# First mixture of a one-core transformer block: row scatters two to a step over eight steps, one more step ahead of the routing product, head attention in smaller parts

## The chip, the core and the metric

The kernel runs on one core of one Trainium2 chip, in fp32. The metric is device time in microseconds for one execution. Within the core the work is spread over five engines: TensorE (PE, with its weight load shown as PEld), VectorE (DVE), ScalarE (ACT), GpSimd (POOL) and SyncE (SP, which here only issues transfers). Each engine runs its own list of instructions in the order in which the program put them; engines wait for one another through semaphores.

## The reference

Input `x` has 8 batches of 512 tokens with 256 features.

```python
x = x + attn_ref(cond_ref(x, bias, mask, ...))      # 1, 2
x = x + ffn_ref(cond2_ref(x, cond, ...))            # 3, 4

# 1 cond_ref: attention with 16 heads of 64 and one key/value head, a bias, a null key
#   and a mask (a query sees only padded keys behind it), then a layer norm
# 2 attn_ref: attention over the 16 heads of each single token
att = softmax(einsum('bthd,btgd->bthg', q, k) / 4)
out = einsum('bthg,btgd->bthd', att, v) @ Wout + bout
# 3 cond2_ref: mixture of 8 experts, the two best for each token
scores = softmax((x @ wt.T + g @ wg.T) / 2)
topk_w, topk_idx = top_k(scores, 2)                 # weights made to sum to 1
y_all = einsum('etm,emh->eth', leaky(x @ w_gate) * (x @ w_up), w_down)   # m = 128
y = sum of topk_w * y_all over the two + leaky(x @ sw_gate) * (x @ sw_up) @ sw_down
# 4 ffn_ref: attention with 16 heads of 16 over all 512 tokens, layer norm,
#   8 experts of 512, one per token, layer norm
```

## The kernel before

**Stages.** Up to some 345 us the kernel does attention 1, in which only the last 128 tokens of each batch have keys (`late_keys`); beside it, in steps, run the routing and the mixture of the first group of batches. From 389 to about 1590 us runs the main loop: attention 4 for all eight batches, with the routing, mixture and head attention of what is still missing threaded in between. From 1590 us on runs the last mixture of experts.

**The main loop.** It has 256 passes called halves, 32 to a batch. A batch has four sets of four heads, a set takes eight halves, and a half does a row tile of 128 tokens for two heads. In each half TensorE makes the score rows for two heads of the set ahead (`pss`, line 1613), whose greatest value VectorE takes (`nmz`, line 1615), and the transposed scores of the current set (`pst`, line 1637), whose exponential ScalarE takes (`pT_s`, line 1638). These tiles share four PSUM banks. `augment` (line 1628) turns the greatest values and subtracts them, once per set; `project` makes queries and keys of a later set; `gather` (`po_s`, line 1660) multiplies weights and values. `divide` takes the sums of a set to SBUF by a small transfer (`sums`, on ACT's queue), takes their reciprocal (line 1684), sends it back by another small transfer (`rr`, line 1685, on SP's queue), and two steps later spreads it with a product on TensorE (`prs`, line 1689). `end` closes a batch: projection (`px_s`), residual, and a layer norm whose power is a POOL instruction (`e_rs`, line 1712).

**Steps at the side.** Routing, mixture and the begin of the next batch are Python generators; each `yield` ends a step. A plan lists them with their number of steps and, for each batch's begin, the half by which it must be done. In every half as many steps are taken as the nearest goal asks for: 73 steps up to half 48 in the kernel before, about 1.5 a half, and 1.14 a half later.

Batches go in four groups of two (q = 0 to 3). `route(b)` works in five steps: load and turn the rows, logits (`pl_r`), softmax, the two best (`oc`, `r_o`), then a product that counts for each token how many tokens before it chose the same expert (`pr`, line 1353). `mixture(q)` makes from the counts a slot for each of the 2 × 1024 choices (line 1379), writes each token's row to its two slots with indirect transfers issued by POOL (`xs`, line 1387: 16 of them a group, each 128 rows), and fetches the weights of the first pairs of tiles (`fetch`, SP). Some steps later `rows(0)` and `rows(1)` load the sorted rows (`xg`, line 1415, on SP's queue; such a load must wait for the last scatter), and `turn`, `widen` and `narrow` run twelve pairs of tiles.

**Heads.** `late_heads` does attention 2 for the last row tile of each batch, 29 steps a batch: `products` multiplies eight blocks of two heads on POOL (line 321, four buffers), and VectorE sums each block three steps later (line 324); this is done twice, for scores and for values. The sums are pinned: VectorE runs them in program order. In the main loop four such steps are taken per half until they run out. The heads of the first batches are done beside `late_keys`.

**The order on an engine.** Instructions that are not pinned may be placed by a scheduler at compile time; on the chip the order is fixed, and an instruction that waits holds all behind it on its engine. This holds for the issue of transfers on SP's queue too.

Of the kernel before, what the change touches and what calls it, by code (L numbers as in the profile page):

```python
# [19 lines left out]
NT = S // P  # L20
# [12 lines left out]
GB = 2  # L33
TILE1_BITS = 7
TILE1 = 1 << TILE1_BITS
TILES1 = ((2 * GB * S - E) // TILE1 + E + 1) // 2 * 2
# [4 lines left out]
def tile_adaln_attn_ffn(ctx: ExitStack, tc: tile.TileContext, a: dict, out: bass.AP):  # L41

    nc = tc.nc
# [64 lines left out]
    xs_d = dram.tile([TILES1 * TILE1, D], F32, name="xs", tag="xs")  # L108
# [5 lines left out]
    with nc.allow_non_contiguous_dma(reason="narrow rows"):  # L114
# [8 lines left out]
        out=before, in_=before, pattern=[[1, P]], compare_op=ALU.is_gt, fill=0.0, base=0, channel_multiplier=-1  # L123
# [127 lines left out]
    oh_done = [0] * B  # L251
# [930 lines left out]
    def alone(dma, key, why):  # L1182

        tc.declare_no_dep(dma.ins, group=key, reason=why)
        tc.add_to_no_dep_group(key, dma.ins)
# [36 lines left out]
    with ExitStack() as ph:  # L1222
# [77 lines left out]
        def route(b):  # L1300


            q, bl = divmod(b, GB)
            if b not in x1:
                load_x1(b)
            yield
            xT = x1Ts[b] = transposed(mk, ps_m, x1[b], "x1T", bufs=2, ps_tag="m")

            nc.sync.dma_start(rows_d[b * S : (b + 1) * S, 0:D].rearrange("(t p) c -> p t c", p=P), x1[b])
            yield  # L1310
            if (b + 1) % GB:
                load_x1(b + 1)
            gb = mk.tile([64, P], F32, name="gb", tag="gb", bufs=1)
            nc.vector.tensor_copy(gb, gT[:, b : b + 1].to_broadcast([64, P]))
            pl = ps_m.tile([P, NT, E], F32, name="pl_r", tag="m")
            for t in range(NT):
                for k in range(KD):
                    nc.tensor.matmul(
                        pl[:, t, :], xT[:, k, t * P : (t + 1) * P], wtT[:, k, :], start=(k == 0), stop=False
                    )  # L1320
                nc.tensor.matmul(pl[:, t, :], gb, wgT, start=False, stop=True)
            m = mk.tile([P, NT], F32, name="r_m", tag="r_m")
            nc.vector.tensor_reduce(m, pl, AX.X, ALU.max)
            sc = mk.tile([P, NT, E], F32, name="r_sc", tag="r_sc")
            nc.vector.tensor_tensor(sc, pl, bc(m, 2, E), ALU.subtract)
            nc.scalar.activation(sc, sc, AF.Exp, scale=0.5)
            nc.vector.tensor_reduce(m, sc, AX.X, ALU.add)
            nc.vector.reciprocal(m, m)
            nc.vector.tensor_tensor(sc, sc, bc(m, 2, E), ALU.mult)
            yield  # L1330
            if bl == 0:
                chosen[q] = mp.tile([P, GB, 2, NT, E], F32, name="oc", tag="oc", bufs=2)
                ranks[q] = mp.tile([P, GB, NT, E], F32, name="rk", tag="rk", bufs=2)
            oc = chosen[q][:, bl]
            mw = sel[b] = mp.tile([P, 2, NT], F32, name=f"mw{b}", tag=f"mw{b}")
            m1 = first_max(mk, sc, rank8, "1", oc[:, 0])
            s2 = mk.tile([P, NT, E], F32, name="r_s2", tag="r_s2")
            nc.vector.scalar_tensor_tensor(s2, oc[:, 0], -2.0, sc, ALU.mult, ALU.add)
            m2 = first_max(mk, s2, rank8, "2", oc[:, 1])
            den = mk.tile([P, NT], F32, name="r_den", tag="r_den")  # L1340
            nc.vector.tensor_tensor(den, m1, m2, ALU.add)
            nc.vector.tensor_scalar(den, den, 1e-20, None, ALU.add)
            nc.vector.reciprocal(den, den)
            nc.vector.tensor_tensor(mw[:, 0], m1, den, ALU.mult)
            nc.vector.tensor_tensor(mw[:, 1], m2, den, ALU.mult)
            both_e = mk.tile([P, NT, E], F32, name="r_o", tag="r_o")
            nc.vector.tensor_tensor(both_e, oc[:, 0], oc[:, 1], ALU.add)
            yield
            sf = sofar1[:, q]
            for t in range(NT):  # L1350
                nc.vector.tensor_tensor(sf[:, t + 1, :], sf[:, t, :], both_e[:, t, :], ALU.add)
            pr = ps_m.tile([P, NT, E], F32, name="pr_1", tag="m")
            nc.tensor.matmul(pr, before, both_e, start=True, stop=False)
            nc.tensor.matmul(pr, every, sf[:, 0:NT, :], start=False, stop=True)
            nc.vector.tensor_copy(ranks[q][:, bl], pr)
            nc.vector.tensor_copy(sf[:, 0, :], sf[:, NT, :])
            yield

        PAIRS = TILES1 // 2
        WAIT = 5  # L1360

        def mixture(q):

            bank = ps_m.tile([P, E], F32, name="pn1", tag="m")
            steer, _, lead = table(mp, bank, sofar1[:, q, 0, :], TILES1, TILE1_BITS, "m_")
            rk, oc = ranks.pop(q), chosen.pop(q)
# [12 lines left out]
            nc.vector.tensor_copy(slot.rearrange("p b c t -> p (b c t)"), sf_)  # L1379
            got, xTs, hs = {}, {}, {}  # L1380

            def scatter(bl):

                xb = x1.pop(GB * q + bl)
                for c in range(2):
                    for t in range(NT):
                        sc_ = nc.gpsimd.indirect_dma_start(  # L1387
                            out=xs_d,
                            out_offset=bass.IndirectOffsetOnAxis(ap=slot[:, bl, c, t : t + 1], axis=0),
                            in_=xb[:, t, :],  # L1390
                            in_offset=None,
                            bounds_check=TILES1 * TILE1 - 1,
                            oob_is_err=False,
                        )
                        alone(sc_, f"xs{q}", "no two tokens have one place")

            def fetch(j):
                w = mk.tile([P, 2, 2, KD, P], F32, name="w_gu", tag="w_gu")
                wd = mk.tile([P, 2, D], F32, name="w_dn", tag="w_dn", bufs=3)
                for u in range(2):  # L1400
                    i = 2 * j + u
                    e = nc.sync.value_load(steer[0:1, 0, i : i + 1], min_val=0, max_val=E - 1)
                    for c, src in enumerate(("w_gate", "w_up")):
                        nc.sync.dma_start(
                            w[:, u, c], a[src][bass.ds(e, 1)].rearrange("e (k p) m -> p (e k) m", p=P)
                        )
                    nc.sync.dma_start(wd[:, u], a["w_down"][bass.ds(e, 1)].rearrange("e m d -> (e m) d"))
                got[j] = w, wd
# [40 lines left out]
                r = 2 * j * TILE1  # L1449
                nc.scalar.dma_start(y1_d[q][r : r + 2 * TILE1, :].rearrange("(u p) c -> p u c", p=P), y1)  # L1450

            scatter(0)
            fetch(0)
            yield
            scatter(1)
            fetch(1)
            for _ in range(WAIT - 1):
                yield
            rows(0)
            rows(1)  # L1460
# [192 lines left out]
        def gather(n, c):  # L1653

            b, g = divmod(n, 4)
            if c == 0:
                pos[n] = ps_o.tile([P, S], F32, name="po_s", tag="o")
            ws = [weights.pop((n, c, pr)) for pr in range(2)]
            for hd in range(4):
                nc.tensor.matmul(  # L1660
                    pos[n][hd * 32 : hd * 32 + 32, :],
                    v_sets[b % 3][:, c, (4 * g + hd) * VW : (4 * g + hd) * VW + 32],
                    ws[hd // 2][:, hd % 2, :],
                    start=(c == 0),
                    stop=(c == NT - 1),
                )
# [77 lines left out]
            if j == 7:  # L1744
                augment(0)

        ROUTE, MIX, BEGIN = 5, WAIT + 2 * PAIRS + 4, 15
        plan = []
        for q in range(B // GB):
            plan.append((64 * q + 16, begin(2 * q + 1), BEGIN))  # L1750
# [13 lines left out]
        for j in range(halves):  # L1764
            n, i, pr = half(j)
            b, g = divmod(n, 4)
            if j % 32 == 0 and b:
                last = end(b - 1)
            m, t, pm = half(j + 8 + LEAD)
            assert pm == pr  # L1770
            both(m, t, n, i, pr)
            for _ in range(4):
                next(late_heads)
            if j % 8 == 8 - LEAD and n + 1 < 4 * B:
                augment(n + 1)
            if j % 8 in (1, 2):
                if j % 8 == 1:
                    after = project(n + 2) if n + 2 < 4 * B else iter(())
                next(after, None)
            if j % 8 in (2, 3, 4, 5):  # L1780
                next(over, None)
            if j % 32 >= 6:
                next(last, None)

            due += max([(c - due) / (by - j) for by, c in goals if by > j and c > due], default=0.0)
            while done < due - 1e-6:
                assert next(side, "end") != "end"
                done += 1
            if pr == 0 and i:
                gather(n, i - 1)  # L1790
            if j % 8 == 7:
                gather(n, NT - 1)
                over = divide(n)
                next(over)
# [273 lines left out]
```

## Time and profile before

| | us |
|---|---|
| median of three runs | 1856.75 (1849.16 to 1860.49) |
| profiled execution | 1837.18 |
| its span | 1835.1 |

| engine | busy us | share of the span |
|---|---|---|
| TensorE | 1568.9 | 85% |
| VectorE | 1031.2 | 56% |
| ScalarE | 583.9 | 32% |
| POOL | 561.3 | 31% |

The mean granted TensorE clock is 0.899. The scatters of the four groups start at 256.8, 542.6, 839.3 and 1132.3 us. The first turn of rows of the mixture (`pt`, line 1423) comes at 283.3 us. The augments, one for each eight halves, come at 401.3, 455.3, 515.6, 589.1, 635.2 and 684.6 us, then 40 us apart and less. The granted clock in windows of 10 us is 0.78, 0.67, 0.50, 0.52 and 1.00 from 540 to 590 us.

How to read the lines further down: a timeline line has start and duration in us, engine, line, operation, output and inputs, shape, the number of instructions taken together, and in brackets the idle time of the engine before it and what ended it. A line of the waits has engine and line that waited, the releaser, and then total us, times, and the longest.

### The profile page before, as it was taken

Reading aid. Unit: us, or ns where it says so; the run is one execution under the profiler, and the core shown is the slowest. Engines: PE = TensorE matmul, PEld = TensorE weight load, DVE = VectorE, ACT = ScalarE, POOL = GpSimd, SP = SyncE. Lnnn points to the kernel's source line nnn. Section 1 sums busy time; section 2 is a strip of 40 time slices with the busy share of each in tenths; the row PEclk is TensorE's granted clock in tenths of the full one; section 3 lists DMA queues with packets and bytes.
Section 4 is the critical chain, followed back from the end, with each engine's and each line's share of the span. In section 5 each row is a group of like instructions: output and inputs, shape, how many; then the busy total and the mean of one; then the engine's idle time right before and its main releaser. Section 6 shows DMA issues by size and latency. Waiting matters only on the chain.

```text
span 1835.1 us, 23467 instructions
## 1 busy us (share of the span) xinstructions
PE 1568.9 (85%) x7720; PEld 880.9 (48%) x7720; DVE 1031.2 (56%) x2709; ACT 583.9 (32%) x1281; POOL 561.3 (31%) x534
## 2 busy tenths in 40 slices
PE   2897888789897999998999899899899899639995
PEld 1664656543433554443554344454433333228884
DVE  3877554356673655555545656545756656225566
ACT  0433323202222332332353332344343343203331
POOL 2444351425445433103001302201201001147775
PEclk9897788867777989998999998999999999959998
DMA  5121236701114531002850102462100000046872
GB/s 167 39 83 35 83 110 201 199 26 38 32 54 144 165 98 38 19 1 92 190 157 30 36 7 66 109 182 67 37 1 7 13 1 14 4 154 212 238 222 66
DMA packets 189460, 157.77 MB, mean 86 GB/s; under 512 B 43214, under 2 KB 173774, under 8 KB 189329
## 3 DMA queue, kind: packets, MB, share of 16 engines
q1 hardware_dynamic: 147520, 109.10, 20.7%
q0 software_dynamic: 13056, 29.67, 5.1%
q10 hardware_dynamic: 28752, 17.41, 3.2%
q8 instruction: 63, 1.03, 0.3%
q14 instruction: 69, 0.56, 0.1%
HBM read 117.00 MB, written 44.21 MB: 88 GB/s over the span
## 4 chain that ended last, share of the span: by engine, by line
PE 54%; DVE 16%; issue 14%; POOL 8%; DMA 4%; ACT 1%; SPq 0%; POOLq 0%; ACTq 0%; DVEq 0%
PE pss L1613 12%; PE po_s L1660 6%; PE pg L1433 5%; PE pq_s L1565 3%; DVE nmz L1615 3%; PE pk_s L1571 3%; POOL pr L321 3%; POOL xs L1387 3%; PE px_s L1700 2%; PE py L1446 2%; PE pst L1637 2%; PE prs L1689 1%; PE pg L1483 1%; PE pv_s L1592 1%; DMA w_gu<-in_w_up_dram 1%
## 5 line engine op out<-in xcount | busy, mean ns | idle before, releaser
L1615 DVE TENSOR_REDUCE nmz<-pss 128x1 f32<-128x512 f32 x512 | 334.3, 685 | 224.2 <-PE pst L1637 188.7
L1638 ACT ACTIVATE pT_s<-pst 128x512 f32<-128x512 f32 x512 | 282.1, 595 | 448.7 <-PE pst L1637 443.3
L1613 PE MATMUL pss<-k_s,q_s 32*128 32x512 f32 x1024 | 360.7, 682 | 42.9 <-DVE nmz L1615 42.9
L1637 PE MATMUL pst<-q_s,k_s 32*128 32x512 f32 x1024 | 339.6, 670 | 4.5 <-DVE nmz L1615 3.6
L1613 PEld LDWEIGHTS pss<-k_s,q_s 32*128 32x128 f32 x1024 | 103.9, 192 | 229.0 <-DVE nmz L1615 104.9
L1660 PE MATMUL po_s<-pT_s,v 128*32 128x512 f32 x1024 | 165.6, 633 | 8.0 <-ACT pT_s L1638 8.0
L1278 POOL DMA_INDIRECT yg<-y,slot x64 | 66.4, 1038 | 301.7 <-DMA y<-y 170.7
L321 POOL TENSOR_TENSOR pr<-qk 128x512 f32<-128x512 f32 x72 | 89.8, 1282 | 103.5 <-DVE qk L299 67.2
L1433 PEld LDWEIGHTS pg<-xT,w_gu 128*128 128x128 f32 x768 | 95.6, 201 | 40.4 <-ACT xT L1424 17.1
L1433 PE MATMUL pg<-xT,w_gu 128*128 128x128 f32 x768 | 102.7, 289 | 13.3 <-ACT xT L1424 6.9
L321 POOL TENSOR_TENSOR pr<-at,v_h 128x512 f32<-128x512 f32 x72 | 90.5, 1288 | 67.1 <-DVE at L336 38.9
L1637 PEld LDWEIGHTS pst<-q_s,k_s 32*128 32x128 f32 x1024 | 96.8, 190 | 19.6 <-DVE nmz L1615 9.5
L1387 POOL DMA_INDIRECT xs<-x,slot x64 | 63.4, 991 | 126.1 <-DVE slot L1379 108.0
L1888 PE MATMUL ph<-xTj,w 128*128 128x256 f32 x368 | 85.7, 387 | 0.0
L1211 POOL DMA_INDIRECT ids<-token_id,pi x32 | 31.7, 992 | 174.0 <-DVE pi L1208 157.8
L1902 PE MATMUL py<-w,h_e 128*128 128x256 f32 x368 | 83.5, 380 | 1.4 <-issue 1.4
L1891 ACT ACTIVATE h_e<-ph,b 128x256 f32<-128x256 f32 x92 | 43.5, 473 | 108.8 <-PE ph L1888 105.1
L1888 PEld LDWEIGHTS ph<-xTj,w 128*128 128x128 f32 x368 | 71.5, 195 | 10.3 <-ACT xTj L1876 0.2
L1438 DVE TENSOR_TENSOR hh<-hh,pg 128x256 f32<-128x256 f32 x48 | 20.2, 420 | 97.0 <-ACT hh L1437 97.0
L1902 PEld LDWEIGHTS py<-w,h_e 128*128 128x128 f32 x368 | 68.2, 190 | 10.1 <-issue 1.8
L1565 PE MATMUL pq_s<-yT,wqp 128*128 128x512 f32 x128 | 68.7, 663 | 0.9 <-DVE hh L1439 0.7
L1712 POOL TENSOR_TENSOR e_rs<-e_ve,mhalf 128x4 f32<-128x4 f32 x8 | 8.9, 1108 | 192.9 <-DVE e_ve L1710 192.7
(298 smaller groups left out, 2604.2 us busy)
## 6 DMA issues: line engine op xcount, KB each, us to landing
w<-in_w_dram SPq DMA_DIRECT2D x46, 512.0 KB
w_gu<-in_w_gate_dram SPq DMA_DIRECT2D x96, 128.0 KB
w_gu<-in_w_up_dram SPq DMA_DIRECT2D x96, 128.0 KB
w_dn<-in_w_down_dram SPq DMA_DIRECT2D x96, 128.0 KB
xg<-xs SPq DMA_DIRECT2D x48, 256.0 KB
y<-y ACTq DMA_DIRECT2D x48, 256.0 KB
rows<-xr SPq DMA_DIRECT2D x8, 544.0 KB
x<-x SPq DMA_DIRECT2D x8, 512.0 KB
```

The lines of the kernel that those rows point to most:

```text
L321: nc.gpsimd.tensor_tensor(pr, x, y, ALU.mult)
L1278: nc.gpsimd.indirect_dma_start(out=yg[t][:, c, :], out_offset=None, in_=y1_d[grp], in_offset=bass.IndirectOffsetOnAxis(ap=yi[:, c, t : t + ...
L1387: sc_ = nc.gpsimd.indirect_dma_start(out=xs_d, out_offset=bass.IndirectOffsetOnAxis(ap=slot[:, bl, c, t : t + 1], axis=0), in_=xb[:, t, :] ...
L1433: nc.tensor.matmul(pg[:, c, u, :], w[:, u, c, k, :], xT[:, k, u, :], start=(k == 0), stop=(k == KD - 1))
L1565: nc.tensor.matmul(pq, wqp[:, k, gs], yT[:, k, :], start=(k == 0), stop=(k == KD - 1))
L1613: nc.tensor.matmul(pss, qs[n][r, t * P : (t + 1) * P], ks[n][r, :], start=True, stop=True)
L1615: yield lambda: nc.vector.tensor_reduce(nmz[n % 2].rearrange("p t (h r) -> p t h r", h=4)[:, t, h, HD : HD + 1], pss, AX.X, ALU.max, negat ...
L1637: nc.tensor.matmul(pst, ks[n][r, c * P : (c + 1) * P], qs[n][r, :], start=True, stop=True)
L1638: yield lambda: nc.scalar.activation(pT[:, u, :], pst, AF.Exp)
L1660: nc.tensor.matmul(pos[n][hd * 32 : hd * 32 + 32, :], v_sets[b % 3][:, c, (4 * g + hd) * VW : (4 * g + hd) * VW + 32], ws[hd // 2][:, hd % ...
L1888: nc.tensor.matmul(ph_, w1[:, k, c * P : (c + 1) * P], xT[:, k, :], start=(k == 0), stop=(k == KD - 1))
L1902: nc.tensor.matmul(py[:, u, :], h[:, c, u * P : (u + 1) * P], w2[:, c, :], start=(c == 0), stop=(c == 3))
```

## The change

`route` gets one more `yield`, between the running sums and the counting product. `mixture` begins with a `yield` of its own. Its scatters are no longer issued in two blocks of eight (a batch each) but two to a step over eight steps (a row tile of 128 tokens with its two choices), with the weight fetches at the first and the fifth; two steps after the last scatter step, where there were four after the second block, the rows are asked for. The constants that tell the plan the number of steps follow (ROUTE 5 to 6, MIX 33 to 38). In the main loop the head steps are no longer taken four at a time ahead of the side steps: two come ahead, and behind the side steps and `gather` two more, or one more once the head of the fourth batch is done.

```diff
@@ route
                 nc.vector.tensor_tensor(sf[:, t + 1, :], sf[:, t, :], both_e[:, t, :], ALU.add)
+            yield
             pr = ps_m.tile([P, NT, E], F32, name="pr_1", tag="m")
@@
-        WAIT = 5
+        WAIT = 12
 
         def mixture(q):
 
+            yield
             bank = ps_m.tile([P, E], F32, name="pn1", tag="m")
...
-            def scatter(bl):
-
-                xb = x1.pop(GB * q + bl)
+            xb = [x1.pop(GB * q + bl) for bl in range(GB)]
+
+            def scatter(k):
+
+                bl, t = divmod(k, NT)
                 for c in range(2):
-                    for t in range(NT):
-                        sc_ = nc.gpsimd.indirect_dma_start(
...
+                    sc_ = nc.gpsimd.indirect_dma_start(
...
@@
-            scatter(0)
-            fetch(0)
-            yield
-            scatter(1)
-            fetch(1)
-            for _ in range(WAIT - 1):
+            for k in range(GB * NT):
+                scatter(k)
+                if k % 4 == 0:
+                    fetch(k // 4)
+                yield
+            for _ in range(WAIT - GB * NT - 3):
                 yield
             rows(0)
             rows(1)
@@
-        ROUTE, MIX, BEGIN = 5, WAIT + 2 * PAIRS + 4, 15
+        ROUTE, MIX, BEGIN = 6, WAIT + 2 * PAIRS + 2, 15
@@ main loop
             both(m, t, n, i, pr)
-            for _ in range(4):
+            for _ in range(2):
                 next(late_heads)
...
             if pr == 0 and i:
                 gather(n, i - 1)
+            for _ in range(1 if oh_done[2 * GB - 1] == NT else 2):
+                next(late_heads)
             if j % 8 == 7:
```

## The prediction

> **What bounds the kernel now.** I read the busy times first, then the shares of the chain that ended last, then the waits of TensorE, and last the timeline around each wait that this change touches.
>
> ```profile
> PE 1568.9 (85%) x7720; PEld 880.9 (48%) x7720; DVE 1031.2 (56%) x2709; ACT 583.9 (32%) x1281; POOL 561.3 (31%) x534
> PE 54%; DVE 16%; issue 14%; POOL 8%; DMA 4%; ACT 1%; SPq 0%; POOLq 0%; ACTq 0%; DVEq 0%
> PE pss L1613 <- DVE nmz L1615: 42.9, 43, 10.0
> PE prs L1689: 15.3, 3
> ```
>
> The last two are from the waits (us in total, times, longest) and from who waited for the DMA of line 1685. TensorE is the bound: busy 85% of 1835.1 us. A change to scatters and steps saves time only where TensorE stands still, or runs at a lower granted clock because it stood still. Its idle time in the stretch with head attention (388 to 700 us) is about 32 us. So three places matter: the scatters of group 1 (543 to 563 us), the ends of the scatters of groups 2 and 3 (860 and 1153 us), and the routing products near 500 us.
>
> Group 1, timeline of POOL, VectorE and TensorE:
>
> ```profile
> 542.59 1.05 POOL L1387 DMA_INDIRECT xs<-x,slot  x1 [0.32 <-DVE slot L1379]
> ...
> 562.15 0.98 POOL L1387 DMA_INDIRECT xs<-x,slot  x1 [0.30 <-issue]
> 563.14 6.11 POOL L321 TENSOR_TENSOR pr<-at,v_h 128x512 f32<-128x512 f32 x5
> 564.45 0.69 DVE L324 TENSOR_REDUCE oh<-pr 128x32 f32<-128x512 f32 x1 [14.70 <-POOL pr L321]
> 549.21 1.22 PE L1613 MATMUL pss<-k_s,q_s 32*128 32x512 f32 x1 [3.03 <-DVE nmz L1615]
> 565.79 1.22 PE L1613 MATMUL pss<-k_s,q_s 32*128 32x512 f32 x1 [10.04 <-DVE nmz L1615]
> ```
>
> Sixteen scatters hold POOL for 20.6 us (1.29 us from one to the next). The head's product stands behind them, the reduce of that product blocks VectorE for 14.7 us, the row maxima behind it come late, and TensorE stops for 3.0 and 10.0 us.
>
> Group 2, the chain of waits:
>
> ```profile
> 858.51 2.42 DMA xs<-x,slot
> 860.94 0.38 SPq L1415
> 861.36 0.47 SPq L1415
> 861.95 2.69 DMA rr<-sums
> 864.68 2.07 PE prs L1689 x2
> ```
>
> No heads are left here, so POOL's block itself costs nothing. But the two loads of scattered rows (L1415) wait in SP's queue for the last scatter to land, and behind them in that queue stands the small transfer of the softmax reciprocals (L1685). Those were computed at 848.6; their transfer goes out at 861.95. TensorE stands idle 4.68 us before L1689, and as long at group 3:
>
> ```profile
> 864.68 2.07 PE L1689 MATMUL prs<-rr,cst 128*128 128x512 f32 x2 [4.68 <-DMA rr<-sums]
> ```
>
> **The change, part by part.** Nothing is removed: the same 64 scatters, transfers and products are issued. What changes is their place. I read it from the order in which the changed kernel's instructions stand on each engine.
>
> *Groups 2 and 3.* POOL still gets 16 scatters in a row, since no other POOL work lies between; they start when the slots are ready and take 20.6 + 2.4 us to land. Rows(0) now comes nine side steps after the first scatter, before five: at some 1.25 steps a half (1.14 before) and 5 us a half that is 36 us instead of 22, so the loads find their rows written; and in SP's order the transfer of reciprocals now stands ahead of both. So the idle times go: 4.68 + 4.58 us. The granted clock after them was 0.75, 0.50, 0.50 and 0.55 in the four 2-us windows from 862 to 870 and 1.00 after 870: about 5.2 us of work at half clock, so 2.6 to 2.8 us lost each time. Together 7.3 + 7.4 = 14.7 us. Against it: the power of the layer norm (L1712, POOL) stood right behind the scatters at 859.5 and 1152.5 and can be the next late thing (0 to 3 us in all), and the pair weights are fetched with a slightly shorter lead. I take −12.5 (ends −14.7 and −1.5, the latter if the next wait takes nearly all of it).
>
> The Trainium skill, "TensorE: Matmul & The Clock Gate", section "The HAM clock gate", says that after an idle window of about 3.4 us the clock is halved and comes back after about 3.4 us of sustained work. By that page each of these stalls would be worth an estimated 4.6 + 1.7 = 6.3 us, and the sum below would be −12 and not −14; the trace disagrees, with 5 us at half clock here and 12 us at 0.50 to 0.52 after the 10-us stop at 566.
>
> *Group 1.* POOL's order is now 4 scatters, 3 products, 4 scatters, 2 products, 8 scatters, then products: smaller blocks, but the last is still 8 × 1.29 = 10.3 us, and on VectorE the reduce that needs the first product behind it stands directly behind the earlier reduces. POOL has 20.6 + 5 × 1.28 = 27 us of work there, in halves that took 31 us before. Going through the order by hand, VectorE waits about 5, 4 and 10 us in place of 14.7, and TensorE, which has up to four score banks of slack, about 0, 3 and 11 in place of 3 + 10 + 2. I take 0; the ends are −15 − 6 = −21 (blocks wholly covered, and some 12 us at half clock no longer lost) and +6 (a stall per block).
>
> *Group 0* runs beside late-key attention (before 388 us). The layer norm power (L89), for which VectorE waited 9.1 and 7.0 us there, no longer stands behind eight scatters at once, but the first turned rows come later: rows(0) comes six to eight side steps later, at ten steps a unit 0.6 to 0.8 unit, and the mixture starts about one group of instructions later. TensorE's turn of the rows waited 7.5 us for them before. The 12 pairs behind it take 5.1 us each, the transfer engines 82 to 99% busy. I take +3; the ends are −4 and +20 (the whole delay of the rows shows at the end of the stage).
>
> *Routing.* The product of line 1353 stood idle 6.48 us for the chosen experts, with some 2.6 us of half clock behind it:
>
> ```profile
> 502.63 0.61 PE L1353 MATMUL pr<-r_o,before 128*128 128x32 f32 x2 [6.48 <-DVE r_o L1347]
> ```
>
> It gets one more step of distance, but in TensorE's order it still stands two halves behind the logits, with fewer reduces ahead of it on VectorE. I take −4 (ends −9 and 0).
>
> *Heads.* Steps per half fall from 4 to 3 once the fourth batch's head is done (about half 7). Five heads of 29 steps end at half 36 now; (145 − 28)/3 = 39 more halves makes it 46. The work is the same: 16 × 1.28 = 20.5 us of POOL, about 14.5 us of VectorE and 4.9 us of TensorE a head. Eight halves with heads took 54.0, 60.3, 73.5, 46.0 and 49.5 us; the same stage without them took 40.1, 40.0, 43.7, 33.5 and 32.3. So heads cost 93.7 us in about 39 halves, 2.4 us a half (3.7 at worst, 29.8/8). If the cost goes with the work it is 0; I take 0 (the ends are in the rivals).
>
> Sum: −12.5 + 0 + 3 − 4 + 0 = −13.5, say −14 us on the profiled execution's 1837.2 us, −0.76%. That execution is 1.05% under the median of the runs shown, so the forecast on the median is 1856.75 × (1 − 0.0076) = 1842.6. Its own range, from the smaller ends above, is 1833 to 1853.
>
> **Rivals.**
>
> *The smaller parts really hide the scatters.* Head steps now come in two lots a half, one of them behind the side steps, so the products find POOL between the scatters. For: the 14.7-us wait of VectorE has no other cause. Against: eight scatters in a row remain in POOL's order. It would save the 21 us of group 1 besides: −35, so 1821. If the calmer order lifts the granted clock too (0.72 to 0.77 from 350 to 600 us, 0.9 to 1.0 later), it is more.
>
> *Slower: the longer stretch of heads.* If what a half pays for heads is fixed (the stop of VectorE at a POOL product, and the low clock that follows) and not by the step, 9.7 more halves pay 2.4 to 3.7 us: +23 to +36, net +9 to +22, so 1866 to 1879. For: the cost of a head by this count, 93.7/5 = 19 us, is far above its 4.9 us of TensorE. Against: with three products' reduces in place of four a half, each stop should be shorter. It decides by the cost of a half with 3 steps: at 93.7/48.7 = 1.9 us heads cost what they did, from (93.7 + 14)/48.7 = 2.2 the gain is gone, from 2.6 the kernel is slower by over 1%.
>
> *The change at groups 2 and 3 doesn't do what the order suggests.* The reciprocals go out in time, but L1712 or the weights stop TensorE as long: −1.5, so 1855.
>
> **How the numbers follow.** Chances: forecast 0.38, hidden scatters 0.24, longer stretch 0.30, next wait 0.08. Predicted is the forecast, 1842. About 1% is what a measurement of this kernel can tell from no change: the bounds are 1838.2 and 1875.3. Faster takes a third of the forecast's chance (0.13) and nearly all of the second (0.23): 0.36. Slower takes two thirds of the third, with group 0's +20 as a helper: 0.21. The rest, 0.43, is within. The range runs from 1815 (the second case, with some clock gained) to 1878 (the third case's far end).
>
> **What would show it.** At 860 and 1153 us: L1689 without idle time, the DMA of L1685 landing before the last scatter. At group 1: TensorE's idle at L1613 summing to about 15 us again; under 5 would mean the second case. Near 500 us: the wait of L1353 down to a few us. Heads' last product near half 46, with eight halves taking 47 to 55 us between half 36 and half 46 if the third case holds, and 37 to 45 if it doesn't. The first turn of rows later than 283 us by under 10 us. Wrong at the root would be a wait of TensorE that is not in the list above, or a start of the main loop more than 20 us later.

## The result, and the profile after

| | before | after |
|---|---|---|
| median of seven runs, us | 1856.75 | 1840.92 |
| ratio, 95% interval | | 0.9922 (0.9896 to 0.9948) |
| median on a second chip, beside each other, us | 1853.53 | 1833.76 |
| ratio there, 95% interval | | 0.9884 (0.9847 to 0.9921) |
| profiled execution, span, us | 1835.1 | 1839.2 |

One of the seven runs of after took 1960.76 us at a granted clock of 0.786; the ratio is taken without this slow run. The change makes the kernel 0.8 to 1.2% faster: 15.8 us on the runs of the forecast, which was 1842. But the two traces differ the other way, by 4 us. So the first question is whether the trace of before shows a usual execution. The first lines of the page of after, busy times and the shares of the chain:

```profile
PE 1570.0 (85%) x7720; PEld 878.3 (48%) x7720; DVE 1018.7 (55%) x2709; ACT 584.3 (32%) x1281; POOL 561.0 (31%) x534
PE 67%; DVE 12%; issue 6%; POOL 5%; DMA 4%; ACT 1%; another core or an unknown queue 1%; SPq 0%; POOLq 0%; DVEq 0%; ACTq 0%
```

The work is the same. New in the chain is a releaser that the profile can't name. At group 1 the timeline of after has this on POOL, VectorE and TensorE:

```profile
536.70 3.70 POOL L321 TENSOR_TENSOR pr<-qk 128x512 f32<-128x512 f32 x3
...
545.45 2.48 POOL L321 TENSOR_TENSOR pr<-qk 128x512 f32<-128x512 f32 x2
...
558.14 2.48 POOL L321 TENSOR_TENSOR pr<-qk 128x512 f32<-128x512 f32 x2
546.75 0.69 DVE L324 TENSOR_REDUCE at<-pr 128x32 f32<-128x512 f32 x1 [2.81 <-POOL pr L321]
559.45 0.69 DVE L324 TENSOR_REDUCE at<-pr 128x32 f32<-128x512 f32 x1 [10.22 <-POOL pr L321]
562.00 1.22 PE L1616 MATMUL pss<-k_s,q_s 32*128 32x512 f32 x1 [11.37 <-DVE nmz L1618]
513.65 0.61 PE L1354 MATMUL pr<-r_o,before 128*128 128x32 f32 x2 [2.79 <-DVE r_o L1347]
```

The eight scatters that still stand in a row ahead of 558.14 hold the reduce for 10.22 us and TensorE for 11.37 us; the counting product of the routing waits 2.79 us where it waited 6.48. At group 2 the wait for the reciprocals is gone, and this stands there instead, in the timeline of after:

```profile
847.39 0.75 DVE L1570 TENSOR_SCALAR q_s<-pq_s,bqp 128x512 f32<-128x512 f32 x1 [5.03 <-remote]
856.83 0.42 DVE L1707 TENSOR_TENSOR y<-px_s,y 128x256 f32<-128x256 f32 x1 [8.68 <-remote]
856.91 1.09 ACT L1641 ACTIVATE pT_s<-pst 128x512 f32<-128x512 f32 x2 [12.50 <-remote]
858.36 1.22 PE L1616 MATMUL pss<-k_s,q_s 32*128 32x512 f32 x1 [9.87 <-DVE nmz L1618]
```

The add at 856.83 needs a product that TensorE had ended at 841.6, and ScalarE's exponential needs scores that were ready at 845.6. Both start within 0.1 us of each other, after 8.7 and 12.5 us of idle time, while POOL went on issuing scatters to 854. TensorE then stands still for 9.87 us. Group 3 has the same (12.76 us on TensorE). The first trace of before has no such stop.

The stretches used below are cut at the augments: set 1 runs from the first augment to the second, and so on to set 31. The steps at the side move between sets when the plan changes, so a set of one kernel need not hold the same work as that of another. Where it matters, a stretch is taken apart into TensorE's idle time, the time lost to the granted clock (each busy stretch times what its clock lacks to 1.00), and the rest, which is work at full clock. The rest adds up to 1425 to 1440 us in each of the fourteen traces. These parts are estimates, since the ends of products are modelled in the profile.

### The profile page after: what moved, and what is told of

Its sections match the earlier page's. It is cut to its first block, busy times and chain, and to the rows that moved or that the text cites. A ratio compares the mean times of both kernels' runs of the same rounds, so it can differ in the third digit from the quotient of the medians.

```text
span 1839.2 us, 23454 instructions
## 1 busy us (share of the span) xinstructions
PE 1570.0 (85%) x7720; PEld 878.3 (48%) x7720; DVE 1018.7 (55%) x2709; ACT 584.3 (32%) x1281; POOL 561.0 (31%) x534
## 4 chain that ended last, share of the span: by engine, by line
PE 67%; DVE 12%; issue 6%; POOL 5%; DMA 4%; ACT 1%; another core or an unknown queue 1%; SPq 0%; POOLq 0%; DVEq 0%; ACTq 0%
PE pss L1616 15%; PE po_s L1663 7%; PE pg L1436 4%; PE ph L1893 3%; PE pq_s L1568 3%; PE py L1907 3%; PE pk_s L1574 3%; PE px_s L1703 3%; DVE nmz L1618 3%; PE py L1449 2%; POOL pr L321 2%; PE pv_s L1595 2%; PE pst L1640 2%; PE prs L1692 2%; PE pg L1486 2%
## 5 line engine op out<-in xcount | busy, mean ns | idle before, releaser
L1616 PE MATMUL pss<-k_s,q_s 32*128 32x512 f32 x1024 | 374.7, 693 | 71.5 <-DVE nmz L1618 70.9
L1640 PE MATMUL pst<-q_s,k_s 32*128 32x512 f32 x1024 | 358.5, 690 | 2.9 <-DVE nmz L1618 1.1
L1616 PEld LDWEIGHTS pss<-k_s,q_s 32*128 32x128 f32 x1024 | 107.6, 196 | 270.0 <-DVE nmz L1618 144.3
L1640 PEld LDWEIGHTS pst<-q_s,k_s 32*128 32x128 f32 x1024 | 102.0, 196 | 17.0 <-issue 10.5
L1907 PEld LDWEIGHTS py<-w,h_e 128*128 128x128 f32 x368 | 68.2, 190 | 10.2 <-issue 1.8
L1568 PE MATMUL pq_s<-yT,wqp 128*128 128x512 f32 x128 | 64.1, 623 | 0.1
L1703 PE MATMUL px_s<-wop,oT_s 128*128 128x256 f32 x256 | 63.6, 395 | 0.0
```

What stands on the lines that cost most here:

```text
L1568: nc.tensor.matmul(pq, wqp[:, k, gs], yT[:, k, :], start=(k == 0), stop=(k == KD - 1))
L1616: nc.tensor.matmul(pss, qs[n][r, t * P : (t + 1) * P], ks[n][r, :], start=True, stop=True)
L1640: nc.tensor.matmul(pst, ks[n][r, c * P : (c + 1) * P], qs[n][r, :], start=True, stop=True)
L1703: nc.tensor.matmul(px, oTs[4 * b + g][:, t * P : (t + 1) * P], wop[:, g, :], start=(g == 0), stop=(g == 3))
L1907: nc.tensor.matmul(py[:, u, :], h[:, c, u * P : (u + 1) * P], w2[:, c, :], start=(c == 0), stop=(c == 3))
```

## The experiments

**The kernel before, traced twice more**, with no edit, on two chips.

> The kernel before, unchanged, traced once more. Its seven timed runs lie between 1849 and 1860 us, its traced execution at 1837, so the trace in hand is 1% faster than what is to be explained. Theory A (the row loads held the reciprocals' transfer): this trace is like the first, TensorE waits 4.6 us ahead of the spreading product near 860 and 1155 us, and the 18 us are spread evenly. Rival B (what the changed trace shows near 845 to 857 us, a stop of VectorE, ScalarE and TensorE of 5 to 12 us while POOL issues scatters, ended by a releaser that the profile calls remote, is in the usual run of the kernel before too, and longer): this trace is at 1849 to 1860 us and has such stops beside its scatters.

> The kernel before, traced on the chip on which the next three run. If the stops of all engines beside the scatters (a releaser that the profile calls remote) belong to the execution and not to the kernel, they are here or not here as they are in the next three traces, and the time against the first trace of the kernel before differs by them: sets 10 and 18 of the main loop take 40 us each without them, 51 with them.

Measured: 1848.93 and 1842.04 us. Both have the stops. The timeline of the first of them, at group 2:

```profile
857.47 0.58 ACT L1676 COPY oT_s<-po_s 128x512 f32<-128x512 f32 x1 [14.26 <-remote]
860.44 1.29 DVE L1615 TENSOR_REDUCE nmz<-pss 128x1 f32<-128x512 f32 x2 [11.01 <-remote]
861.18 1.21 PE L1613 MATMUL pss<-k_s,q_s 32*128 32x512 f32 x1 [13.74 <-DVE nmz L1615]
```

So the wait on which the forecast's largest term rests (4.68 us ahead of the spreading product) is what one execution showed; in these two a stop of 13.7 or 13.2 us of TensorE stands at the same place, and the wait isn't seen. Sets 10 and 18 take 51.0 and 51.4, and 53.1 and 51.4 us, against 40.0 and 40.3 in the first trace. The second trace is 11.8 us longer than the first: 22.1 us in these two sets, less 10 us elsewhere. In all, nine of the fourteen traces of this study have stops with that releaser, and the traces of two chips all have them; the four traces of a third chip have none. They belong to the chip or the execution, not to this change. At group 1 the kernel before has none; three of the other traces have some there (routing step alone, heads alone, and the smaller change below).

**The three parts, one at a time.**

Scatter part alone, on the kernel before:

```diff
-        WAIT = 5
+        WAIT = 12
...
+            yield
...
+            for k in range(GB * NT):
+                scatter(k)
...
-        ROUTE, MIX, BEGIN = 5, WAIT + 2 * PAIRS + 4, 15
+        ROUTE, MIX, BEGIN = 5, WAIT + 2 * PAIRS + 2, 15
```

> The kernel before with the mixture's part alone (a step ahead, two scatters a step over eight steps, rows later); routing and heads as before. Theory A: most of the gain is here, -8 to -14 us against the kernel before. Rival B (heads in smaller parts or the routing step make it): within 4 us of the kernel before.

Measured: 1876.56 against 1845.88 us, ratio 1.0159 (1.0138 to 1.018). Slower, which no theory had. The row loads still stand ahead of the reciprocals on SP's queue, though they are asked for later:

```profile
875.02 0.88 SPq L1417 DMA_DIRECT2D xg<-xs  x2
878.06 0.61 SPq L1687 DMA_DIRECT2D rr<-sums  x1
```

Sets 10 and 18 do fall (44.5 and 44.8 us), but sets 7 to 9 take 123.4 us (before 110.2 in the two later traces) and 15 to 17 take 117.3 (107.8 and 106.7). TensorE hardly waits there. The windows of 1 us and the timeline of this kernel, where the logits of the next group's routing stand (the number after the last counts is the granted clock):

```profile
799.00:800.00 1.00, 1.00 (x9) 0.94 (x8) 0.04 (x1) 0.00 (x0) 0.00 (x0) 1.00 0.00 0
800.00:801.00 1.00, 1.00 (x8) 0.96 (x8) 0.00 (x0) 0.00 (x0) 0.00 (x0) 0.88 0.00 0
801.00:802.00 1.00, 1.00 (x6) 0.98 (x6) 0.00 (x0) 0.00 (x0) 0.00 (x0) 0.50 0.00 0
```

```profile
798.24 0.61 PE L1318 MATMUL pl_r<-wtT,x1T 128*128 128x8 f32 x4
...
800.81 1.02 PE L1318 MATMUL pl_r<-wtT,x1T 128*128 128x8 f32 x4
```

From 800 to 806 us the clock is 0.56, from 806 to 820 it is 0.62, and 0.71 from 820 to 852: a stretch with two batches' logits and counting products in it runs at about two thirds of the clock. Over these 52 us the mean is 0.67, some 17 us less work than at full clock. The fall itself is nothing special to this kernel (the last section counts it in all traces); here the clock stays low for longer. TensorE loses 18.0 us to the clock in sets 7 to 9 and 13.0 in 15 to 17, where the kernel before on the same chip loses 10.4 and 6.9. That is 7.6 and 6.1 us of the 13.2 and 9.5 us that these sets are longer. Why it stays low for longer was not taken apart.

Routing step alone:

```diff
+            yield
             pr = ps_m.tile([P, NT, E], F32, name="pr_1", tag="m")
...
-        ROUTE, MIX, BEGIN = 5, WAIT + 2 * PAIRS + 4, 15
+        ROUTE, MIX, BEGIN = 6, WAIT + 2 * PAIRS + 4, 15
```

> The kernel before with the one more step ahead of the routing product alone. Theory A: -4 us (-9 to 0), the wait of the counting product near 500 us falls from 6.5 to some 3 us. Rival: 0, the waits come elsewhere.

Measured: 1851.68 us, ratio 1.002 (0.9997 to 1.0044). No gain. The counting product near 500 us waits 1.60 us in place of 6.41, but at group 1 TensorE waits 16.67 us for a sum of the heads, where its longest wait was 10.0: the waits come elsewhere, as the rival had it. The trace has stops at groups 2 and 3, after which TensorE has stood still for 14.21 and 14.07 us.

Heads alone:

```diff
-            for _ in range(4):
+            for _ in range(2):
                 next(late_heads)
...
+            for _ in range(1 if oh_done[2 * GB - 1] == NT else 2):
+                next(late_heads)
```

> The kernel before with the head steps alone taken as in the change (two ahead, two or one behind the side steps). Theory A: 0 (-4 to +4 us). Rival (a half pays for heads, not a step): +23 us. Rival (smaller parts let the products in between): -10 us or more.

Measured: 1843.11 us, ratio 0.9974 (0.9945 to 1.0003). Against the trace of before of the same chip, sets 1 to 3 fall from 188.3 to 167.4 us and sets 4 to 6 rise from 136.5 to 156.6: 20.9 us early, 20.1 us given back.

The parts add up to +1.5%, and the whole is 0.8% faster. So the parts don't simply add.

**Two parts at a time.** Routing and heads without the scatter part; scatter and routing without the heads (the diffs are those above, put together).

> The changed kernel with the scatter part undone. If the parts add up: -0.1%. If the gain of 0.8% needs the scatters in small blocks (theory A: row loads no longer ahead of the reciprocals): no gain, -0.3 to +0.3%. If heads and routing make it: -0.8%.

Measured: 1839.92 against 1826.18 us, ratio 1.01 (1.0061 to 1.014). Slower, which no theory had. SP's queue and TensorE at group 2 in its timeline, on the chip without stops:

```profile
849.79 0.61 SPq L1686 DMA_DIRECT2D rr<-sums  x1
863.34 0.90 SPq L1416 DMA_DIRECT2D xg<-xs  x2
865.86 1.12 PE L1424 MATMUL pt<-ident,xg 128*128 128x128 f32 x4 [9.24 <-DMA xg<-xs]
```

The reciprocals go out ahead of the row loads here, and in the trace of the routing step alone (864.94 and 871.98 us), with the old scatters and the old wait; with the scatter part alone, whose rows come later, they do not. So it is the routing step that changes their order, by moving the mixture against the sets. But nothing is won, for TensorE runs on to the turn of the rows and waits there for 9.24 us (9.37 at group 3), since the rows are still asked for after five steps.

> The changed kernel with the heads undone (four steps ahead again): scatter part and routing step together. If the parts add up, it is 1.6% + 0.2% = 1.8% slower than the kernel before. If the routing step takes away what made the scatter part alone slow (the halved clock of 800 to 845 us, in the stretch in which two batches are routed), it is within 0.6% of the kernel before, and the sets 8 and 9 of the main loop (eight halves each) take some 65 us together as in the changed kernel, not 80.

Measured: 1813.15 against 1826.18 us, ratio 0.9938 (0.9917 to 0.9959). Faster. Sets 8 and 9 take 67.1 us (80.4 with the scatter part alone), and sets 10 and 18 take 34.2 and 33.6, where they took 40.0 and 40.3 in the first trace of before, which has no stops either. Most of this is work that went elsewhere. The windows of the two sets (after the length: TensorE's busy time and number of products), first before, then this kernel:

```profile
837.90:877.90 40.00, 34.12 (x172) 15.97 (x170) 21.06 (x47) 11.84 (x22) 16.68 (x17) 0.90 0.46 148
1130.90:1171.20 40.30, 34.46 (x171) 16.06 (x169) 21.03 (x48) 11.89 (x22) 16.71 (x17) 0.89 0.44 138
821.20:855.40 34.20, 29.04 (x146) 13.18 (x146) 21.58 (x57) 10.17 (x18) 16.83 (x17) 0.90 0.38 124
1108.70:1142.30 33.60, 28.55 (x146) 12.83 (x145) 21.73 (x58) 10.20 (x19) 16.71 (x17) 0.91 0.39 126
```

TensorE is idle 11.7 us in the two sets of before and 10.2 us here, but it is busy 11.0 us less, for the first turns and products of the mixture (8 `pt` and 16 `pg` a set) now lie in a later set. The wait that is left at group 2 in its timeline:

```profile
848.62 1.06 POOL L1715 TENSOR_TENSOR e_rs<-e_ve,mhalf 128x4 f32<-128x4 f32 x1
849.71 0.48 DVE L1727 SCALAR_TENSOR_TENSOR xr<-xr,e_rs,b_bc 128x256 f32<-128x256 f32 x1 [3.74 <-POOL e_rs L1715]
851.25 1.22 PE L1616 MATMUL pss<-k_s,q_s 32*128 32x512 f32 x1 [4.40 <-DVE nmz L1618]
```

This is the layer norm's power behind the sixteen scatters, the next late thing. TensorE waits 4.40 us for it here and 4.28 at group 3, about as long as for the reciprocals before (4.68 and 4.58).

**Against the stops**, on the chip of the two runs just told. The slots copied out a row tile at a time, so that POOL's scatters spread:

```diff
-            nc.vector.tensor_copy(slot.rearrange("p b c t -> p (b c t)"), sf_)
+            sv = sf_.rearrange("p (b c t) -> p b c t", b=GB, c=2)
...
                 bl, t = divmod(k, NT)
+                pin(nc.vector.tensor_copy(slot[:, bl, :, t], sv[:, bl, :, t]))
```

> The changed kernel with the slots copied out a row tile at a time, in the step that scatters it, so that POOL gets its scatters two by two over eight steps in groups 2 and 3 also, where they now run 16 in a row. Theory C (the stop of all engines of 8 to 10 us near 850 and 1150 us comes from the burst of 16 indirect writes): the two stops go, with 6 to 8 us of half clock behind each, -20 to -30 us against the changed kernel. Rival (each scatter stops the engines as much wherever it lies): no gain. Rival (a late row load takes their place): slower by up to 10 us.

And the first weight loads asked for late:

```diff
-                if k % 4 == 0:
-                    fetch(k // 4)
+                if k == GB * NT - 1:
+                    fetch(0)
                 yield
+            fetch(1)
```

> The changed kernel with the first weight loads of a group asked for at the last scatter and a step later, not at the first and fifth. Theory D (the stop near 850 and 1150 us is the scatters' traffic together with the weight loads): the stops shrink from 8 to 10 us to under 4, -10 to -20 us. Rival (the scatters alone make it): they stay, 0 to +6 us.

Measured: 1814.37 us, ratio 0.9947 (0.9924 to 0.997), and 1814.67 us, ratio 0.9949 (0.9925 to 0.9974). Neither tells anything of the stops, since no trace of this chip has one. The whole change itself was not run on this chip, so the nearest are scatter and routing without the heads (0.9938), and the two edits beside each other: neither wins or loses by more than the intervals. The spread scatters lie hardly further apart in the trace (826 to 849 us), but at group 2 the layer norm's power now slips in between them:

```profile
840.22 1.06 POOL L1716 TENSOR_TENSOR e_rs<-e_ve,mhalf 128x4 f32<-128x4 f32 x1
```

The wait of 4.40 us for it is gone, and TensorE is idle 3.6 us in sets 10 and 18 in place of 10.2. They take 29.8 and 30.4 us, and set 11 takes 50.4 instead of 43.1, so nothing is won in all.

**The whole change, the change without its heads, and a smaller change that keeps only what was found**, on one chip. The last has, on the kernel before, the routing step and rows three steps later, with the scatters in two blocks of eight:

```diff
+            yield
             pr = ps_m.tile([P, NT, E], F32, name="pr_1", tag="m")
...
-        WAIT = 5
+        WAIT = 8
...
-        ROUTE, MIX, BEGIN = 5, WAIT + 2 * PAIRS + 4, 15
+        ROUTE, MIX, BEGIN = 6, WAIT + 2 * PAIRS + 4, 15
```

> The changed kernel again, on one chip with the two that follow. 0.6 to 0.9% faster than the kernel before. Sets 10 and 18 take some 34 us each if there are no stops.

> The changed kernel with the heads undone, beside the whole change. If the heads in smaller parts add to it (group 1 and the sets before it are shorter): the whole change is 0.2% or more faster than this. If the longer stretch of heads gives all of it back: the two are within 0.1%.

> The kernel before with the routing step and with the rows asked for three steps later; the scatters stay in two blocks of eight, the heads as before. In its order the reciprocals' transfer stands ahead of the row loads in groups 2 and 3, as in the changed kernel. Theory E (two things are needed, the routing step puts the reciprocals ahead of the row loads, the later rows take away the wait of the turn for them, 9.2 us where only the routing step was made): sets 10 and 18 fall to 34 us each as in the changed kernel, -0.4 to -0.8%. Rival (the scatters in small blocks make the gain): within 0.3% of the kernel before, sets 10 and 18 at 40 us or more.

Measured against 1853.53 us: whole 1833.76, ratio 0.9884 (0.9847 to 0.9921); without heads 1838.46, ratio 0.9909 (0.9875 to 0.9943); smaller change 1851.17, ratio 0.9981 (0.9955 to 1.0008). The whole change gains more than was expected, the smaller one less than its theory and no more than its rival. All have stops here, so sets 10 and 18 stay at 45.8 to 47.5 us in the three (53.1 and 51.4 in the kernel before on this chip), and 34 us was not reached. The smaller change gets the same there as the whole one, but its sets 1 to 3 take 181.9 us (170.9 without heads, 161.8 whole) and its sets 15 to 17 take 109.9 (103.9 and 103.9). At group 1 of the smaller change TensorE's timeline has a long wait and a short one, and without the heads' part three short ones; first the smaller change, then the other:

```profile
559.20 2.05 PE L1690 MATMUL prs<-rr,cst 128*128 128x512 f32 x2 [11.44 <-DMA rr<-sums]
...
568.11 0.48 PE L342 MATMUL poT<-ident,oh 128*128 128x128 f32 x1 [4.86 <-DVE oh L324]
```

```profile
542.11 1.22 PE L1616 MATMUL pss<-k_s,q_s 32*128 32x512 f32 x1 [5.43 <-DVE nmz L1618]
...
552.11 2.07 PE L1640 MATMUL pst<-q_s,k_s 32*128 32x512 f32 x2 [2.61 <-DVE nmz L1618]
558.99 0.48 PE L342 MATMUL poT<-ident,oh 128*128 128x128 f32 x1 [4.81 <-DVE oh L324]
```

These waits add up to 16.3 and 12.9 us, and over sets 1 to 6 TensorE is idle 43.4 us in the smaller change and 33.0 without heads; 6.0 of these 10.4 us go to a lower clock. At 559.20 the reciprocals are late again: they were computed by 542.1, and their transfer stood behind weight loads on SP's queue until 558.99. ScalarE has two stops of that nameless releaser in this stretch (9.57 and 8.90 us), so part of the difference may belong to the chip.

So the two blocks of eight don't do for most of the gain (0.9981 against 0.9909, intervals apart). The two kernels also differ by the mixture's own first step and by one step more to the rows; that it is the scatters two to a step is likely, but not shown by itself. Group 1, where head products share POOL with the scatters, is one place of the difference. Sets 7 to 9 and 11 to 17 are another: 9.0 us shorter, of which 7.8 is work that lies elsewhere. Whether the heads add to scatter and routing (0.9884 against 0.9909) the intervals don't tell.

## Why the prediction was right, and where it was not

The time came out as forecast, the reason only in part. Each stretch as the mean of the two traces of before with stops, and of the two of after (both with stops). The column "idle and clock" is what TensorE's idle time and the time lost to the clock changed; what is left of the difference is work that moved:

| stretch | before, us | after, us | difference | idle and clock | forecast's term |
|---|---|---|---|---|---|
| up to the first augment | 396.6 | 406.6 | +10.0 | +6.2 | +3 (group 0) |
| sets 1 to 3 | 189.6 | 161.8 | -27.8 | -10.4 | -4 (routing), 0 (group 1), heads |
| sets 4 to 6 | 134.9 | 147.4 | +12.5 | +1.1 | heads |
| sets 10 and 18 | 103.5 | 93.4 | -10.1 | -3.4 | -12.5 (groups 2 and 3) |
| sets 7 to 9, 11 to 17 | 359.5 | 365.2 | +5.7 | +3.2 | none |
| set 19 to the end | 659.5 | 665.4 | +5.9 | +2.3 | none |

*Groups 2 and 3.* This step failed. The sets did become shorter by about what was forecast: -10.1 us here, and -12.5 between two traces without stops (80.3 us in the first trace of before, 67.8 with scatter and routing). But 6.7 and 8.6 us of that are work that lies in other sets now. What TensorE won in waits and clock is 3.4 us with stops and 3.8 without them, where 12.5 was forecast; the agreement of the sizes is chance. The reciprocals do go out ahead of the row loads and their wait is gone, but the power of line 1712, priced at 0 to 3 us in all, takes 4.40 and 4.28 us of TensorE where there are no stops. That is the prediction's own last rival (the next wait stops TensorE as long), which had a chance of 0.08. Nor do the reciprocals go ahead because the rows come later: the routing step alone turns that order, and then the rows are late by 9.24 us. The later rows take that second wait away. The change needs both; the forecast had credited one.

*Group 1.* The waits came as the order was read (VectorE 2.81 and 10.22 us for 5, 4 and 10; TensorE 11.37 for about 14 in all), so the rival that the scatters would be hidden by the heads' smaller parts is not what happened. But the term of 0 was mis-sized, together with the -4 of the routing: sets 1 to 6 hold heads, routing and group 1, and their idle time and clock fall by 9.2 us (10.0 between the traces without stops). Two thirds of that is clock: 6.3 us with stops, 6.7 without. The forecast took a lower clock to follow from TensorE standing still; the traces show it behind the logits' products too, without idle time, and no term had this. What raised the clock in these sets was not taken apart further. The routing step by itself gave nothing (sets 1 to 6: 326.1 against 324.8 us).

*Heads.* The term of 0 held: ratio 0.9974, interval across 1. Three steps instead of four from about half 7 leave some 16 of the 145 steps for later; in the traces 40 of the 80 products of the main loop lie in sets 1 to 3 where there were 49. By the forecast's own 93.7 us for all of them that is about 10 us, against 20.9 won and 20.1 lost, so half of the shift is something else. The slower rival, that a half pays for heads whatever it does, would have cost 23 us or more and falls with the ratio. But its sign came: the eight halves of set 6 take 48.7 us in both traces of after, within the 47 to 55 that the prediction named for it. The sign couldn't tell the rivals apart, since sets 1 to 3 became shorter by more than that.

*Group 0.* +3 was forecast; the first pair of traces has +3.1 (401.3 to 404.4). The table's +10.0 has 4.7 from one trace of before in which the loop began 9.4 us early, so it is no better measure.

*What was missing.* The change puts 80 steps up to half 48 where there were 73, and 1.25 a half later where there were 1.14, and the forecast had no term for that. It can be in the row of sets 7 to 9 and 11 to 17 and in part of the last. With the scatter part alone it was far more, through the clock. Nor does the list of waits have the stops with the nameless releaser, which the prediction's own sign (a wait that is not in the list) would call wrong at the root; the kernel before has them too.

*A reading of the clock.* The prediction sets 12 us at half clock after the 10-us stop (566 to 578 us) against the rule that it quotes. TensorE was busy for 9.37 of these 12 us, so the work was not sustained there, and that row decides nothing.

The sum of -14 us against 15.8 measured is therefore luck: groups 2 and 3 gave some 9 us less than forecast, group 1 with the routing some 5 us more, and the rest lies in stretches without a term or open. What stays open: the traced executions of the table differ by 4 us only (1.0 of it in idle time and clock), the medians by 16 and 20; the two traces without stops, on chips that need not be the same and without the heads' part, differ by 23 (16.7 of it in idle time and clock). Of the traces of before, the first lies 19.6 us below the median of its runs, the second 3.1 above, the third 11.5 below (9.4 of it by the early begin of its loop); of those of after one is the median and one lies 8.4 above. Which row of the table holds the rest in the usual execution no trace tells.

## What to carry to other kernels

Where a transfer of a small result shares a queue with a load that waits for others, look for two things at once: which of them stands ahead, and when the load's data are ready; removing one wait alone showed the other here (9.2 us). Then look who stands behind both: with both gone, the next wait took 4.40 us in place of 4.68. When steps move, the length of a stretch tells little by itself; count the products in it and its idle time before calling a shorter stretch a gain (here 12.5 us shorter, 3.8 won). Before pricing a wait of a few us from one trace, trace the same kernel again: the wait of 4.68 us was in one trace of three. And when a plan's steps are moved, try the parts alone and in pairs: here one part was 1.6% slower alone, one made no difference, and the two together were 0.6 to 0.9% faster.

## What the runs showed of the hardware

While POOL issues sixteen indirect writes of 128 rows, 1.29 us apart, VectorE and ScalarE stood still in nine traces, among them all eight of two chips, for up to 17.1 us. In the trace of after their inputs had been finished by TensorE long before (841.6 and 845.6 us). Both started again at nearly the same time (860.44 and 860.48 us in the kernel before, 856.83 and 856.91 in after); TensorE stopped behind them for up to 14.2 us. The same kernel, scatter and routing, has 45.8 and 46.0 us in sets 10 and 18 on a chip with the stops and 34.2 and 33.6 on one without. What releases the engines was not found.

The granted clock fell from 1.00 to 0.50 at 801 us in the scatter part alone although the timeline shows TensorE without idle time from 788 to 806 us; it was issuing the logits' products of 8 columns each (L1318, four in 0.61 us). The Trainium skill, "TensorE: Matmul & The Clock Gate", section "The HAM clock gate", ties half clock to an idle window of about 3.4 us. Here no idle window stood ahead of the drop, only about 3 us of narrow products, and the measurement decides. It is no single case. In the main loops of the fourteen traces 81 blocks of logits start at full clock, and in 69 the clock falls to 0.50 within 6 us, in 60 of them with no idle time of TensorE from 4 us before the block to the fall. To compare: of 3191 moments at full clock in the same loops, taken every 2 us, with no idle TensorE within 4 us and no logits within 6 us, 5 are followed by such a fall. So a block of narrow products was mostly followed by half clock as an idle stretch is; in 12 of the 81 it was not.
